# The bias of V on every other tile: from a TensorE matmul to VectorE's way out of PSUM, with a re-planned order

## The chip, the core and the metric

The kernel runs on one core of one Trainium2 chip. The metric is the device time in microseconds (us) of one execution; below is the median of several runs. The profile shows one execution, with the engines TensorE (PE; its weight loads are PEld), VectorE (DVE), ScalarE (ACT), GpSimd (POOL), and SyncE's DMA queue (SP).

## What is computed

One pre-norm layer of graph attention with a residual, on 16 graphs (batches) of 1024 nodes and 512 features, 8 heads of 64. All batches share one sparse adjacency matrix. All values are float32.

```python
h = jnp.maximum(_layernorm(x, axis=-1), 0.0)            # x: (16, 1024, 512)
q = (h @ Wq + bq).reshape(b, n, H, HD)                  # H, HD = 8, 64
k = (h @ Wk + bk).reshape(b, n, H, HD)
v = (h @ Wv + bv).reshape(b, n, H, HD)
scores = jnp.einsum('bihd,bjhd->bhij', q, k) / jnp.sqrt(jnp.float32(HD))
mask = jnp.where(adj == 0, jnp.float32(-1000000000.0), jnp.float32(0.0))
weights = jax.nn.softmax(scores + mask[None, None, :, :], axis=-1)
out = jnp.einsum('bhij,bjhd->bihd', weights, v)
x = x + out.reshape(b, n, H * HD)
```

## The kernel before

Only neighbours are computed. At the start the kernel counts each node's neighbours, ranks the nodes by that count (`degree`, `keys`, `rank_of`, `ranks`, `list_of`, `spots`), and puts them into eight tiles of 128 rows. Tile 0 holds the nodes with the longest lists, tile 7 those with the shortest. `CAPS` says how many neighbours a tile has at most (11, 8, 6, 5, 4, 3, 3, 2); the rest of the longest lists goes into "pieces", a ninth tile called -1. Tiles are taken in the order 7, 6, ..., 0 (`TILES`).

For each batch there are two halves of work.

*Projections.* A tile of x is loaded in ranked order by an indirect DMA of GpSimd (`load_x`). VectorE forms mean and variance (`stats`, `variance`, `shift`), GpSimd the power -1/2 (`power`). ScalarE norms (`norm`), TensorE flips (`flip`), ScalarE copies the flip to SBUF (`unflip`). TensorE then projects K, V and Q (`proj_kv`, `queries`). In `project` a projection is one bfloat16 matmul of `chosen` (ones in three rows) with `bias` (the bias of each projection as three bfloat16 parts that add up to it), and then four float32 matmuls, which the profile shows as eight. The three parts are made at the start by `round` on ScalarE and `remain` on GpSimd, from the bias vectors that `load_b` fetches. ScalarE takes K and V from PSUM into the tile `kvt` (`evict_kv`; the pool pkv has two PSUM banks), and SP stores it in DRAM (`store_kv`). Batch 0's rows are first projected unranked, as "batch -1" (tile names with `first`), while the ranking is still under way.

*Attention.* The slots of a tile are worked off in 14 units of up to four (`UNITS`; unit 10 is the first of tile 0, 11 the pieces, 12 and 13 the rest of tile 0). GpSimd gathers neighbours' rows of K and V by indirect DMAs (`gather`; a tile's own rows come through SP). VectorE multiplies K with the query from PSUM (`multiply`) and sums by heads (`score`), ScalarE does the exponential (`exponent`). V is weighed mostly on ScalarE, with eight activations per slot (`weigh_s`), partly on VectorE (`weigh_v`). Slots are added on VectorE or GpSimd (`fold`, `join`) and, for tile 0, on TensorE (`add_up` into the PSUM tile acc; `more` and `pass_on` bring the pieces' sums home, the matmul p_more). In the last batch most tiles are added up on TensorE. Then come `row_sums`, `scale`, `residual` and `put_out`, an indirect DMA of GpSimd.

The attention of batch b runs beside the projections of batch b+1, with three K/V tables in DRAM.

Each engine has one queue, in order. The order is made by a planner (`Plan.ordered`) in the program that builds the kernel: each operation has a length and delay (`LENGTHS`), a place (due time) from `AT` with small shifts from `FINE`, the operations it comes after, and the buffers it uses (`POOLS`). The planner takes, whenever an engine is free, the ready operation with the earliest place. So a changed place changes the order of all five queues, and nothing else.

Of the kernel before, what the change touches and what calls it, by code (L numbers as in the profile page):

```python
# [25 lines left out]
F32 = mybir.dt.float32  # L26
# [47 lines left out]
    load_x=106.07, stats=-2.83, variance=-3.87, power=-87.25, shift=-9.66, norm=-4.89, flip=-7.74, unflip=-31.23, proj_kv=-1.94,  # L74
    evict_kv=38.12, queries=-1.19, own=55.32, gather=-1.08, score=6.6, exponent=29.51, row_sums=-147.93, share=2.3,
    weigh_v=-2.68, weigh_s=90.78, fold=-2.21, join=-4.72, add_up=-1.79, direct_residual=35.08, direct_out=32.8, more=-13.17,
    pass_on=-2.39, sums=-5.19, scale=0.94, residual=-6.43, put_out=4.53, seen=40.3, zero=-27.7, zero_rate=2.38, ahead=59.92,
    early=0.74, early2=0.64, early3=0.06, first=-83.71, first_rate=7.94, v_late=15.02, key_row=-167.51, rank_row=-115.31,
    rank_d=-95.84, rank_a=-60.26, ranks=19.11, ends=25.44, list_of=68.48, tell=-159.3, spread=-73.79, others=69.47,
    spots=-98.99, long_rows=-53.11, long_0=-52.44, long=-81.28, longest=-48.97, count=59.77, pieces=-68.14, setup=-27.7,  # L80
    parts=-24.89,
)
FINE = {
    ('list_of', 5): 4.08, ('spread', 2): -8.9, (0, 'fold', 11, 2, 2): -4.64, (0, 'fold', 7, 1, 1): -1.63,
    (0, 'fold', 9, 1, 1): 4.81, (0, 'gather', 0, 1): -2.77, (0, 'gather', 10, 2): 1.19, (0, 'gather', 9, 3): -3.73,
    (0, 'join', 7): -0.85, (0, 'join', 9): 7.45, (0, 'multiply', 6): 10, (0, 'put_out', 0, 0): -1.85,
    (0, 'queries', 0, 0): -1.28, (0, 'queries', 0, 1): -0.25, (0, 'scale', 0, 1): -8.55, (0, 'weigh_s', 6, 0): 2.5,
    (1, 'fold', 1, 2, 1): 18.39, (1, 'fold', 10, 2, 2): 2.32, (1, 'fold', 11, 2, 2): -1.59, (1, 'fold', 12, 1, 1): 5.31,
    (1, 'fold', 8, 2, 2): -2.33, (1, 'norm', 2): 1.1, (1, 'norm', 3): -1.68, (1, 'proj_kv', 1, 0): -0.18,
    (1, 'proj_kv', 2, 1): -0.39, (1, 'proj_kv', 4, 1): -0.64, (1, 'proj_kv', 5, 0): 0.79, (1, 'queries', 0, 0): -0.05,  # L90
    (1, 'scale', 0, 0): -11.49, (1, 'score', 0): 0.65, (1, 'stats', 6): -0.58, (1, 'weigh_v', 12): -2.31, (2, 'flip', 6): -1.85,
    (2, 'gather', 6, 1): 9.99, (2, 'gather', 9, 0): 2.04, (2, 'multiply', 7): -1.89, (2, 'pass_on', 0): -4.55,
    (2, 'proj_kv', 5, 1): 4.27, (2, 'stats', 6): -0.96, (2, 'store_kv', 3): 0.05,
}
POOLS = dict(x=17, h=2, pht=2, hT=11, pkv=2, kvt=3, q=2, q0=1, g=6, acc=2, o=1)
GROUP = 2
JOIN = False


LENGTHS = dict(  # L100
    zeros=(0.15, 2.0, 0.0), load_w=(0.2, 2.5, 3.0), load_b=(0.6, 2.2, 0.0), load_adj=(0.2, 2.5, 1.5),
    setup=(1.0, 0.1, 0), add_bias=(0.22, 0.2, 0), join_acc=(0.602, 0.13, 0),
# [14 lines left out]
LENGTHS["fold", "POOL"] = LENGTHS["residual", "POOL"] = (1.43, 0.0, 0)  # L117
LENGTHS["gather", "SP"] = (0.1, 3.0, 1.36)
# [3 lines left out]
SHARED = ("fold", "join",  "weigh_v", "residual", "scale", "power")  # L122
# [3 lines left out]
BY_TILE = ("load_x", "stats", "norm", "flip", "unflip", "proj_kv", "evict_kv", "store_kv", "proj_q", "evict_q", "store_q")  # L126
BY_HOME = ("queries", "row_sums", "residual", "put_out", "scale", "more", "pass_on", "copy_q", "seen")
# [129 lines left out]
def planned(B):  # L257
# [17 lines left out]
    for j in range(3):  # L275
        known = [("remain", j - 1)] if j else [("parts_at",)] + [("load_b", name) for name in names]
        add(("round", j), "ACT", AT["parts"] + j, known)
        if j < 2:
            add(("remain", j), "POOL", AT["parts"] + j, [("round", j)])
# [42 lines left out]
    for n in range(-NT, tiles):  # L322
# [19 lines left out]
        for w in range(2):  # L342
# [4 lines left out]
            add(("proj_kv", n, w), "PE", e, ready, [("hT", n), ("pkv", n, w)], length=3.436 if n == -NT else None)  # L347
# [4 lines left out]
            add(("evict_kv", n, w), "ACT", e + AT["evict_kv"], ready, [("pkv", n, w), ("kvt", n)])  # L352
        ready = [("evict_kv", n, w) for w in range(2)]
        if n >= 0:
            add(("store_kv", n), "SP", p, ready, [("kvt", n)])
            continue
        add(("store_kv", n), "POOL", p, ready + [("ranks",)] + ([("store_kv", n - 1)] if n > -NT else []), [("kvt", n)])

# [5 lines left out]
    for k in range(units):  # L364
# [6 lines left out]
        q = ("q", b, t)  # L371
        if q not in q_of:
            p = i + AT["queries"]
            if t >= 0:
                ready = [("unflip", n)] + ([("round", 2), ("setup", 0), ("load_w", "q")] if b == 0 else [])
                add(("queries", b, t), "PE", p, ready, [("hT", n), q])
                if t == 0:
                    add(("copy_q", b), "ACT", p + 0.5, [("queries", b, 0)], [q, ("q0", b)])
            else:
                add(("queries", b, t), "PE", p, [("copy_q", b)] + ([("slots", 0)] if b == 0 else []), [q, ("q0", b)], length=0.86)  # L380
            q_of[q] = ("queries", b, t)
# [40 lines left out]
        elif without_tensor(b, B, home) or joined(b, B, home):  # L422
# [5 lines left out]
            summed = added  # L428
        else:
# [40 lines left out]

def is_own(u, s):

    t, first, _ = UNITS[u]
    return t >= 0 and first + s == 0


def shares_in(b, B, t):
    return t in SHARES and (b < B - 1 or t in LAST_DIRECT)


def by_vector(b, B, u):

# [853 lines left out]
```

## Time and profile before

| | |
|---|---|
| median of 11 runs | 1672.31 us (1668.26 to 1677.72) |
| the profiled execution's own time | 1675.62 us |
| its span, first to last instruction | 1673.9 us |
| granted TensorE clock, mean of the span | 0.984 |
| PE, DVE, ACT, POOL busy | 1595.8, 1482.9, 1470.5, 1272.7 us |
| DMA | 531.73 MB, 318 GB/s over the span |
| period of a steady batch | 97.7 us (p_more of tile 0 from 1280.6 to 1378.3) |

In the page's rows a slice is a fortieth of the span, and a digit the busy share in tenths. A row of a group gives line, engine, operation, output<-inputs with shapes, count | busy us, mean ns of one | idle time before it, and what ended it. A row of waits reads "engine line <- releaser: us in total, times, longest". A row of the timeline has start and duration in us, and in brackets the idle time before it. "issue" is idle time in which the engine waited for nothing that the profile shows; GpSimd has 0.30 us of it at nearly each indirect DMA.

### The profile page before, as it was taken

Reading aid. Unit: us, or ns where it says so; the run is one execution under the profiler, and the core shown is the slowest. Engines: PE = TensorE matmul, PEld = TensorE weight load, DVE = VectorE, ACT = ScalarE, POOL = GpSimd, SP = SyncE. Lnnn points to the kernel's source line nnn. Section 1 sums busy time; section 2 is a strip of 40 time slices with the busy share of each in tenths; the row PEclk is TensorE's granted clock in tenths of the full one; section 3 lists DMA queues with packets and bytes.
Section 4 is the critical chain, followed back from the end, with each engine's and each line's share of the span. In section 5 each row is a group of like instructions: output and inputs, shape, how many; then the busy total and the mean of one; then the engine's idle time right before and its main releaser. Section 6 shows DMA issues by size and latency. Waiting matters only on the chain. (4 is left out here: it accounts for less than half of the span.)

```text
span 1673.9 us, 19582 instructions
## 1 busy us (share of the span) xinstructions
PE 1595.8 (95%) x4295; PEld 737.1 (44%) x4295; DVE 1482.9 (89%) x2019; ACT 1470.5 (88%) x5479; POOL 1272.7 (76%) x1184
## 2 busy tenths in 40 slices
PE   6989999999999999999999999999999999999687
PEld 3444444444444444444444444444444444444233
DVE  6788989889898998989899898989989898998986
ACT  4359988989989898998989899898989989899976
POOL 2767777687887878788787887878787887877755
PEclk9999999999999999999999999999999999999788
DMA  6498989899898999999899998989999898999894
GB/s 229 137 333 299 336 308 338 296 355 326 317 347 304 363 325 348 327 318 348 306 357 319 349 329 306 344 321 356 323 346 332 311 350 315 358 321 332 283 330 162
DMA packets 150741, 531.73 MB, mean 318 GB/s; under 512 B 19916, under 2 KB 19916, under 8 KB 150616
## 3 DMA queue, kind: packets, MB, share of 16 engines
q0 software_dynamic: 109840, 390.70, 65.7%
q1 hardware_dynamic: 40776, 139.71, 22.9%
q8 instruction: 36, 0.59, 0.1%
q14 instruction: 89, 0.73, 0.1%
HBM read 429.51 MB, written 100.82 MB: 317 GB/s over the span
## 5 line engine op out<-in xcount | busy, mean ns | idle before, releaser
L1057 ACT ACTIVATE g<-g,weights 128x64 f32<-128x64 f32 x4696 | 1162.4, 339 | 8.0 <-DVE weights L1044 4.2
L1021 POOL DMA_INDIRECT g<-kv,index x608 | 640.1, 1053 | 247.1 <-issue 166.9
L799 PE MATMUL pq<-wq,hT 128*128 128x512 f32 x1024 | 460.3, 592 | 0.0
L1031 DVE TENSOR_TENSOR g<-g,pq 128x1536 f32<-128x1536 f32 (+2 forms) x208 | 385.7, 1871 | 82.3 <-PE pq L799 67.2
L799 PE MATMUL pk<-wk,hT 128*128 128x512 f32 x960 | 432.8, 594 | 0.0
L799 PE MATMUL pv<-wv,hT 128*128 128x512 f32 x960 | 432.3, 593 | 0.0
L1035 DVE TENSOR_REDUCE weights<-g 128x24 f32<-128x1536 f32 (+2 forms) x224 | 421.0, 1895 | 0.5
L799 PEld LDWEIGHTS pq<-wq,hT 128*128 128x128 f32 x1024 | 194.7, 190 | 218.9 <-issue 215.3
L799 PEld LDWEIGHTS pk<-wk,hT 128*128 128x128 f32 x960 | 183.2, 191 | 210.0 <-issue 206.6
L799 PEld LDWEIGHTS pv<-wv,hT 128*128 128x128 f32 x960 | 183.1, 191 | 204.6 <-issue 200.9
L1062 DVE TENSOR_TENSOR g<-g 128x512 f32<-128x512 f32 (+1 forms) x301 | 261.5, 873 | 12.4 <-ACT g L1057 11.8
L1137 POOL DMA_INDIRECT out_dram<-x,perm x128 | 147.1, 1149 | 36.9 <-issue 25.4
L744 POOL DMA_INDIRECT x<-in_x_dram,perm x128 | 141.4, 1105 | 35.4 <-issue 34.8
L1039 ACT ACTIVATE weights<-weights 128x24 f32<-128x24 f32 (+2 forms) x224 | 49.0, 219 | 104.4 <-DVE weights L1035 103.2
L1084 PE MATMUL acc<-g,ident 128*128 128x512 f32 x170 | 90.4, 646 | 35.4 <-DVE g L1062 17.1
L1062 POOL TENSOR_TENSOR g<-g 128x512 f32<-128x512 f32 x90 | 115.0, 1278 | 5.1 <-ACT g L1057 1.4
L1051 DVE TENSOR_TENSOR g<-g,weights 128x512 f32<-128x512 f32 x149 | 104.2, 700 | 0.6
L1134 POOL TENSOR_TENSOR x<-x,o 128x512 f32<-128x512 f32 x67 | 85.9, 1281 | 13.1 <-DVE o L1125 8.8
L779 ACT ACTIVATE h<-x,shift,rstd 128x512 f32<-128x512 f32 x120 | 91.1, 806 | 3.0 <-DMA x<-in_x_dram,perm 3.0
L753 DVE BATCH_NORM_STATS2 st<-x 128x6 f32<-128x512 f32 x120 | 81.9, 682 | 2.4 <-DMA x<-in_x_dram,perm 2.4
L786 PEld LDWEIGHTS pht<-ident,h 128*128 128x128 f32 x512 | 60.4, 141 | 53.3 <-issue 34.4
L786 PE MATMUL pht<-ident,h 128*128 128x128 f32 x512 | 73.4, 276 | 5.0 <-ACT h L779 4.8
(236 smaller groups left out, 1116.1 us busy)
## 6 DMA issues: line engine op xcount, KB each, us to landing
g<-kv SPq DMA_DIRECT2D x128, 512.0 KB, 6.4
kv<-kvt SPq DMA_DIRECT2D x120, 512.0 KB, 4.9
g<-kv,index POOLq DMA_INDIRECT x608, 6.7
adj<-in_adj_dram SPq DMA_DIRECT2D x8, 512.0 KB, 8.5
x_first<-in_x_dram SPq DMA_DIRECT2D x8, 256.0 KB, 8.3
x<-in_x_dram,perm POOLq DMA_INDIRECT x128, 5.9
out_dram<-x,perm POOLq DMA_INDIRECT x128, 5.4
wk<-in_L_gnn_Wk_dram SPq DMA_DIRECT2D x1, 1024.0 KB, 8.7
```

Source lines behind the costliest of these rows:

```text
L744: nc.gpsimd.indirect_dma_start(out=X[n][:], out_offset=None, in_=x_rows, in_offset=on(ap=perm[:, t : t + 1], axis=0), element_offset=b * N * D
L779: nc.scalar.activation(HN[n], X[n], AF.Relu, bias=shift, scale=scale)
L786: nc.tensor.transpose(PH[n][:, c, :], hn[:, ts(c, P)], ident)
L799: nc.tensor.matmul(pt, HT[n][:, c, :], W[name][:, c, :], start=(apart and c == 0), stop=(not apart and c == DC - 1))
L1021: nc.gpsimd.indirect_dma_start(out=G[i][:, s].rearrange("p j d -> p (j d)"), out_offset=None, in_=KV[b % len(KV)][:], in_offset=on(ap=inde ...
L1031: nc.vector.tensor_tensor(k, k, Q[b, t][:, None, :].to_broadcast([P, count, D]), ALU.mult)
L1035: nc.vector.tensor_reduce(weights[:, w, :], heads(G[i][:, :count, 0, :]), AX.X, ALU.add)
L1051: nc.vector.tensor_tensor(v, v, own.to_broadcast([P, n, H, HD]), ALU.mult)
L1057: nc.scalar.activation(v[:, h, :], v[:, h, :], AF.Identity, scale=weights[:, c + s, h : h + 1])
L1062: engine.tensor_tensor(v[:, 0:n], v[:, 0:n], v[:, first : first + n], ALU.add)
L1084: nc.tensor.matmul(ACC[b, home], owner_t if t < 0 else ident, v[:, s, :], start=(u == parts_of(home)[0] and s == 0), stop=(u == parts_of(h ...
L1137: nc.gpsimd.indirect_dma_start(out=out_rows, out_offset=on(ap=perm[:, t : t + 1], axis=0), in_=X.pop(b * NT + TILES.index(t))[:], in_offse ...
```

## The change

V's bias is left out of TensorE's matmuls for the tiles 7, 5, 3 and 1 of batches 1 to 15 (`BIAS_V`; the keys are places in `TILES`). Instead the bias of V is spread once over 128 partitions by one matmul (`spread_bias`), copied into SBUF (`copy_bias`), and added by VectorE as it takes these V tiles from PSUM. The other V tiles and K and Q stay as they were. The first `round` is planned to come after the first `power`. `AT` and `FINE` have new values throughout, so all queues are reordered, and the pool of x tiles has 16 buffers instead of 17. `PAIRED`, `FETCH`, and the GpSimd form of the bias (`bias_v`) come with the code and are switched off; of them only a column of `found0`, one more column of `p_list` and two copies of one column at the start remain.

```diff
-POOLS = dict(x=17, h=2, pht=2, hT=11, pkv=2, kvt=3, q=2, q0=1, g=6, acc=2, o=1)
+POOLS = {'x': 16, 'h': 2, 'pht': 2, 'hT': 11, 'pkv': 2, 'kvt': 3, 'q': 2, 'q0': 1, 'g': 6, 'acc': 2, 'o': 1}
...
+BIAS_V = {0: 'DVE', 2: 'DVE', 4: 'DVE', 6: 'DVE'}
+PAIRED = ()
+FETCH = False
...
+LENGTHS["evict_kv", "DVE"] = (0.602, 0.13, 0)
...
-        known = [("remain", j - 1)] if j else [("parts_at",)] + [("load_b", name) for name in names]
+        known = [("remain", j - 1)] if j else [("parts_at",), ("power", -NT // 2)] + [("load_b", name) for name in names]
...
-            add(("evict_kv", n, w), "ACT", e + AT["evict_kv"], ready, [("pkv", n, w), ("kvt", n)])
+            by = bias_by(n, "kv"[w])
+            if by == "DVE":
+                ready.append(("copy_bias",))
+            add(("evict_kv", n, w), "DVE" if by == "DVE" else "ACT", e + AT["evict_v" if by == "DVE" else "evict_kv"], ready, [("pkv", n, w), ("kvt", n)])
...
+    if BIAS_V:
+        add(("spread_bias",), "PE", AT["spread_bias"], [("round", 2), ("setup", 0)], [("pkv", "bias")])
+        add(("copy_bias",), "ACT", AT["spread_bias"], [("spread_bias",)], [("pkv", "bias")])
...
+def bias_by(n, name):
+
+    return BIAS_V.get(n % NT, "PE") if n >= 0 and name == "v" else "PE"
...
-            apart = n == -NT
+            apart = n == -NT or bias_by(n, name) != "PE"
             if not apart:
                 nc.tensor.matmul(pt, chosen[:, names.index(name), :], bias, start=True, stop=False)
             for c in range(DC):
-                nc.tensor.matmul(pt, HT[n][:, c, :], W[name][:, c, :], start=(apart and c == 0), stop=(not apart and c == DC - 1))
+                nc.tensor.matmul(pt, HT[n][:, c, :], W[name][:, c, :], start=(apart and c == 0), stop=(n != -NT and c == DC - 1))
...
-            nc.scalar.copy(KVT[n][:, j, :], PT.pop((n, j)))
+            if bias_by(n, "kv"[j]) == "DVE":
+                nc.vector.tensor_tensor(KVT[n][:, j, :], PT.pop((n, j)), bias_rows, ALU.add)
+            else:
+                nc.scalar.copy(KVT[n][:, j, :], PT.pop((n, j)))
+
+        bias_rows = const.tile([P, D], F32, tag="bias_rows", name="bias_rows") if BIAS_V else None
+
+        def spread_bias():
+            PT["bias"] = ps_kv.tile([P, D], F32, tag="pkv", name="p_bias")
+            nc.tensor.matmul(PT["bias"], chosen[:, names.index("v"), :], bias, start=True, stop=True)
+
+        def copy_bias():
+            nc.scalar.copy(bias_rows, PT.pop("bias"))
```

The new `AT` and `FINE` are tables of places (`evict_v` is 0.78, `spread_bias` -5.47) and are not shown; what they do to the order is told where it is used.

## The prediction

> **What bounds the kernel now.** I read the page's busy shares and slices first, then the engines' busy time over three steady batches, then what each engine waited for in one of them, then the timelines of the start and the end.
>
> ```profile
> PE 1595.8 (95%) x4295; PEld 737.1 (44%) x4295; DVE 1482.9 (89%) x2019; ACT 1470.5 (88%) x5479; POOL 1272.7 (76%) x1184
> ...
> PE   6989999999999999999999999999999999999687
> ```
>
> TensorE is full from the fourth slice to two slices before the end. Batches 10 to 12 (from one p_more matmul to the next; columns: stretch, its length, busy us with instructions of PE, PEld, DVE, ACT, POOL, granted clock, DMA share, GB/s):
>
> ```profile
> 1085.00:1182.90 97.90, 96.28 (x262) 44.36 (x261) 88.11 (x114) 91.06 (x343) 79.69 (x73) 1.00 0.93 333
> 1182.90:1280.60 97.70, 96.32 (x262) 44.46 (x261) 88.82 (x114) 90.96 (x343) 78.23 (x72) 1.00 0.94 332
> 1280.60:1378.30 97.70, 96.31 (x263) 44.44 (x262) 88.85 (x114) 91.00 (x343) 78.34 (x72) 1.00 0.92 334
> ```
>
> A batch takes 97.7 us, and TensorE works 96.3 of them. It loses 1.4 in small waits. The waits over two batches (us in total, times, longest):
>
> ```profile
> PE acc L1084 <- DVE g L1062: 1.9, 2, 1.0
> PE acc L1084 <- ACT kvt L814: 0.4, 1, 0.4
> PE acc L1084 <- ACT weights L1039: 0.4, 1, 0.4
> ...
> DVE g L1031 <- PE pq L799: 6.7, 2, 3.4
> ```
>
> TensorE waits once per batch for VectorE's fold of tile 0; VectorE waits 3.4 us per batch for a query. TensorE sets the pace. The Trainium skill speaks against that reading: Perfetto Trace Analysis, Identifying the Most-Contended Engine, calls matmul busy time a bad measure and wants LDWEIGHTS busy instead. By it TensorE stands at 44%, VectorE (89%) is the most contended, and a change that hands VectorE 60 more instructions would lose some of their 36 us. The row decides here: eight matmuls follow each other in 3.43 us without a break, and a shorter list on that queue ends earlier. The rule's point, that VectorE is not far behind, goes into the rivals.
>
> The two ends are different. Start (start us, duration, engine, line, idle before):
>
> ```profile
> 11.04 0.72 ACT L654 ACTIVATE scratch<-scratch,later 128x512 bf16<-128x512 f32 x1 [8.55 <-DMA scratch<-in_L_gnn_bq_dram]
> 11.85 1.15 POOL L659 TENSOR_TENSOR scratch<-scratch 128x512 f32<-128x512 f32 x1 [8.07 <-ACT scratch L654]
> 12.96 0.72 POOL L765 TENSOR_TENSOR before_told<-before_told,minus_half 128x2 f32<-128x2 f32 x1
> 13.03 0.72 ACT L654 ACTIVATE scratch<-scratch,later 128x512 bf16<-128x512 f32 x1 [1.27 <-POOL scratch L659]
> ...
> 13.91 1.52 ACT L779 ACTIVATE h_first<-x_first,before_told 128x512 f32<-128x512 f32 x2 [0.16 <-DVE before_told L769]
> ...
> 14.78 1.97 PE L786 MATMUL pht_first<-ident,h_first 128*128 128x128 f32 x8 [14.78 <-ACT h_first L779]
> ```
>
> The first norm waits for a power on GpSimd that is queued behind the bias arithmetic, and that waits for the bias DMA. End: between the last projection and the last batch's sums TensorE is starved of gathers.
>
> ```profile
> 1573.07 2.05 PE L1084 MATMUL acc<-g,ident 128*128 128x512 f32 x2 [9.62 <-issue]
> ...
> 1596.63 0.60 PE L1104 MATMUL p_more<-more,owner_t 128*128 128x8 f32 x2 [8.35 <-DVE more L1100]
> ```
>
> **The change part by part.** Durations are of one execution: span 1673.9, its own time 1675.62, which is 3.3 above the median of 1672.31. I form the difference against the span and take it off the median.
>
> 1. *Bias matmuls.* V of tiles 7, 5, 3, 1 in batches 1 to 15 loses its matmul with chosen: 15 x 4 = 60. The step from it to the next matmul is 0.216 us (1605.41 to 1605.62 in the end's timeline; the row's 379 ns contains pipeline tail). 60 x 0.216 = 13.0 us, all on TensorE's full queue. One matmul is added in the start to spread the bias (0.2): -12.7.
>
> 2. *Evictions.* 60 copies of 128x512 leave ScalarE (step 0.48 each in the chain: 29 us in all, 1.9 per batch). ScalarE had 6.7 us of slack per batch, so this earns nothing by itself. 60 additions PSUM + SBUF to SBUF come to VectorE. The nearest row has the same operand places:
>
> ```profile
> L1125 DVE TENSOR_TENSOR o<-acc,inv 128x512 f32<-128x512 f32 x22 | 15.1, 685 | 1.6 <-POOL x L1134 1.4 <-PE acc L1084 0.2
> ```
>
>    685 ns, or 0.60 from start to start in a run: 36 us, 2.4 per batch. VectorE goes from 88.6 to 91.0 of a batch that shrinks to about 96, all beside TensorE: I cost it at 0. If the cover went, it would cost up to 36. Each addition is queued behind a multiply or score of up to 2.3 us, and behind it wait a multiply and, through the two pkv banks, the next-but-one projection on TensorE. In the new order the tightest are V of tile 3 (pk of tile 2 and a flip follow: 3.65 + 0.43 = 4.1 us until TensorE wants the bank) and of tile 1 (4.9). In both VectorE's work since the last query (multiply 2.2, score 2.2, one to three pieces of 0.6) is 6 to 6.5 us, while the projection itself comes 7.1 to 7.5 after that query. So VectorE is there first, waits about 1 us, and TensorE does not wait.
>
> 3. *Does the addition block GpSimd?* No row of before shows it. SBUF — State Buffer (the Trainium skill, on the shared port pair) says that a VectorE instruction with two SBUF inputs holds a port pair against GpSimd for its whole length; ours has one in PSUM, so by the rule 0. Against it stands that indirect DMAs on GpSimd take 0.94 us in quiet and up to 1.75 in the timeline. If every addition held one up, GpSimd would lose 60 x 0.69 = 41 us, 2.8 per batch. I take 0, since VectorE's multiplies, which also read PSUM, stand beside 0.94 us gathers; 41 stays the far end.
>
> 4. *Start.* On GpSimd the first power moves ahead of the first remainder, so the constants are ready near 6.5. But ScalarE's order is still first rounding, then the two norms, and that rounding waits for the bias DMA until 11.04. Norms then start at 11.8 instead of 13.9, only the second rounding having been passed: the flip 2.1 earlier. The weights wk are in at 10.4 (issued 1.7, 8.7 to landing), so nothing new is late. Second and third rounding end about as before, and the projection that needs them comes 4 us later. -2.1, at most 8 (not reachable in this order), at least 0 if the lists and gathers, not TensorE, set the first batch.
>
> 5. *New places.* The steady order on TensorE puts tile 0's first sum three projections after the pieces' query where it was five, so it must have its fold early. Counted from the end of the query of tile 0: TensorE reaches it after 3.65 + 3.43 + 0.86 + 3.65 + 0.43 + 3.65 + 3.65 = 19.3 us; VectorE and ScalarE (multiply and score 4.4, three weighed slots 5.8 with two norms of 0.8 between, the pieces' multiply and score 4.4 beside them, fold 1.1 + 0.6) reach it near 16. Later sums have about 4 us in hand as well. So the 1.4 us of waits per batch could go. I take half: 0.6 x 12 batches = -7. Bounds: -18 (all idle of TensorE from 350 to 1550 by the slices of 50 us: 1200 - 1182.1) and +1 us or more per batch where a new order makes new waits.
>
> 6. *x pool 17 to 16.* Loads of x come about one tile later, behind the put_out that frees the buffer. In the new order the load of the next batch's first tile is issued some three units (over 15 us) before its statistics, against 5.9 us to landing: 0; without cover, about 6 us per batch. The other additions (two copies of one column in the start, under 0.2 us each; one more column in p_list) are beside longer work.
>
> 7. *The end.* The same gathers and sums in nearly the same order. The query of tile 1 stands behind one sum instead of two (VectorE waited 4.1 us for it), and the last tile's query is ahead of the last three sums. Between -5 and +5; I take 0.
>
> Sum: -12.7 - 2.1 - 7 = -21.8: span 1652, median 1650.5.
>
> **The rivals.** *Another queue takes over.* In batch 12 GpSimd's busy 78.3 and its waits of 19.0 fill the 97.7; of the waits only these two are more than issue:
>
> ```profile
> 1289.77 1.60 POOL L1021 DMA_INDIRECT g<-kv,index  x1 [1.97 <-ACT h L779]
> ...
> 1300.55 1.00 POOL L1021 DMA_INDIRECT g<-kv,index  x1 [2.10 <-issue]
> ```
>
> So GpSimd needs about 94.0 of a batch for which TensorE will need 95.4. A few slower issues and it is the bound, at 97: then 0.7 x 14 = 10 us is gained and with the start 12: 1660. For: the small margin, DMA busy at 0.93. Against: TensorE ends the waits now.
>
> *Late evictions (slower).* An addition stands behind a multiply that waits for its gather (VectorE's such waits reach 3.3 us); TensorE then waits for the pkv bank. Price: one multiply, 2.3 us, once per batch: 15 x 2.3 = 34 - 14.8 = +20: 1692. It decides from 1 us of new TensorE idle per batch, which cancels 0.86 and the start. For: VectorE's slack falls from 9.1 to 4.4. Against: the windows of part 2, and few gather waits in the steady part.
>
> *The places give all back without that*: the old waits stay and the end loses 5 to 10 us: 1662 to 1669. That TensorE executes the bias anyway is excluded: the order has no such matmul.
>
> **How the numbers follow.** TensorE still bound, waits shrunk or kept: 0.64, 1650.5, its own range 1636 to 1660. Other queue or a worse end: 0.18, 1660 to 1675. Slower: 0.18, 1676 to 1710. A measurement of this kernel tells 0.2% (3.3 us) from no change; below 1669: 0.76, within: 0.06, above: 0.18. The range 1636 to 1677 leaves out about 0.03 below and 0.17 above.
>
> **What would show it.** Right: 60 fewer matmuls with chosen and V (one more for the bias rows), 60 VectorE additions into kvt near 0.69 us, batches of 95.5 to 96.8 us, PE over 99% busy in them, first flip near 12.7. Wrong: a wait of pv or pk for DVE kvt among TensorE's waits; GpSimd without gaps while TensorE has them; a batch of 97.7 or more; a longer stretch from the last projection (1563) to the end than 110 us.

## The result: 39 us faster, 17 us more than predicted

The kernel after takes 1633.17 us (median of 8 runs, 1630.63 to 1640.33) against 1672.31: ratio 0.9769, interval 0.9754 to 0.9784, so 2.3% or 39 us less. The prediction was 1650.5, with a range from 1636 to 1677. The direction is right, but the time lies 3 us below the range: the gain is 39.1 where the sum had 21.8, and the runs below show that most of the reasons for it were not the ones given.

The profiled execution took 1628.2 us (span 1626.5), which is 5.0 below the median. Before's took 1675.62, 3.3 above its own. The two traces therefore differ by 47.4 us where the medians differ by 39.1. From the page after (busy shares, then TensorE in forty slices):

```profile
PE 1570.6 (97%) x4236; PEld 728.5 (45%) x4236; DVE 1524.1 (94%) x2081; ACT 1443.2 (89%) x5420; POOL 1250.5 (77%) x1184
...
PE   7999999999999999999999999999999999999696
```

The steady batches 10 to 12 after (stretch, length, busy us of PE, PEld, DVE, ACT, POOL, granted clock, DMA share, GB/s):

```profile
1046.20:1141.60 95.40, 95.00 (x258) 44.12 (x257) 89.58 (x118) 89.32 (x340) 77.45 (x72) 1.00 0.94 342
1141.60:1237.70 96.10, 94.91 (x257) 44.10 (x256) 92.97 (x119) 89.10 (x340) 76.34 (x73) 1.00 0.93 343
1237.70:1333.50 95.80, 94.99 (x258) 44.13 (x257) 91.62 (x118) 89.18 (x340) 76.44 (x72) 1.00 0.94 342
```

A batch takes 95.8 us instead of 97.7, TensorE is busy 95.0 of them, and VectorE has gone up by about 3 us, ScalarE down by 1.8. The removed and the added work show as the diff says (two rows of groups of after: count | busy, mean ns | idle before):

```profile
L841 PE MATMUL pv<-bias_parts,chosen 128*128 128x512 bf16 x60 | 22.8, 380 | 0.0
...
L859 DVE TENSOR_TENSOR kvt<-pv,bias_rows 128x512 f32<-128x512 f32 x60 | 40.7, 678 | 0.3 <-PE pv L843 0.3
```

An addition costs 678 ns, against the predicted 685. Where the time went is seen best with one marker that means the same work in every kernel, the end of the last K or V projection of a batch. The four stretches of before are 0 to the end of batch 1's, to that of batch 3's, to that of batch 15's, to the end:

```profile
0.00:185.20 185.20, 165.54 (x488) 81.29 (x489) 151.66 (x347) 114.11 (x333) 118.99 (x136) 0.99 0.73 259
185.20:386.20 201.00, 195.11 (x522) 89.99 (x521) 176.08 (x224) 178.83 (x671) 151.67 (x141) 0.98 0.90 324
386.20:1559.80 1173.60, 1155.75 (x3114) 532.09 (x3113) 1065.23 (x1349) 1091.67 (x4123) 936.99 (x848) 1.00 0.93 332
1559.80:1673.90 114.10, 79.40 (x176) 33.76 (x175) 89.93 (x102) 85.88 (x357) 65.06 (x61) 0.81 0.72 258
```

And those of after:

```profile
0.00:179.50 179.50, 164.22 (x480) 79.34 (x481) 158.45 (x351) 111.54 (x329) 116.36 (x133) 1.00 0.72 263
179.50:371.60 192.10, 190.32 (x513) 88.14 (x512) 184.66 (x235) 179.52 (x680) 153.45 (x142) 1.00 0.92 338
371.60:1519.90 1148.30, 1139.07 (x3070) 528.86 (x3068) 1094.64 (x1400) 1069.10 (x4066) 917.10 (x850) 1.00 0.93 341
1519.90:1626.50 106.60, 76.97 (x176) 32.18 (x176) 86.35 (x98) 83.08 (x347) 63.56 (x59) 0.87 0.71 261
```

The start gives 5.7 us, batches 2 and 3 give 8.9, the twelve steady batches 25.3 (2.1 each), and the end 7.5. The steady part can be booked on TensorE's own line, and the booking comes out: 48 bias matmuls x 0.216 = 10.4, idle time down from 17.9 to 9.2 = 8.6, and 6.3 left over in busy time, for which these rows give no cause. That is what the prediction's sum would have written. The experiments ask whether the items of this booking are also causes.

What TensorE waits for has changed. The largest waits in the steady stretch before (us in total, times, longest):

```profile
PE acc L1084 <- DVE g L1062: 11.5, 12, 1.0
PE acc L1084 <- ACT kvt L814: 3.6, 8, 0.6
```

and after, where every wait of this stretch (9.1 us) names ScalarE, most of all the copy of the query of tile 0 (`copy_q`), which the query of the pieces needs:

```profile
PE pq_-1_3911 L1070 <- ACT q L1074: 1.5, 1, 1.5
PE pq_-1_5537 L1070 <- ACT q L1074: 1.4, 1, 1.4
...
PE pk L841 <- ACT kvt L861: 0.6, 2, 0.3
```

### The profile page after: what moved, and what is told of

It reads as the page before. It is cut to its first block, busy times and chain, and to the rows that moved or that the text cites. A ratio compares the mean times of both kernels' runs of the same rounds, so it can differ in the third digit from the quotient of the medians.

```text
span 1626.5 us, 19494 instructions
## 1 busy us (share of the span) xinstructions
PE 1570.6 (97%) x4236; PEld 728.5 (45%) x4236; DVE 1524.1 (94%) x2081; ACT 1443.2 (89%) x5420; POOL 1250.5 (77%) x1184
## 5 line engine op out<-in xcount | busy, mean ns | idle before, releaser
L1093 POOL DMA_INDIRECT g<-kv,index x608 | 640.4, 1053 | 215.6 <-issue 163.9
L1107 DVE TENSOR_REDUCE weights<-g 128x32 f32<-128x2048 f32 (+2 forms) x224 | 422.7, 1889 | 0.7
L843 PEld LDWEIGHTS pv<-wv,hT 128*128 128x128 f32 x960 | 180.3, 190 | 191.4 <-issue 187.6
L1134 DVE TENSOR_TENSOR g<-g 128x512 f32<-128x512 f32 (+1 forms) x301 | 253.6, 844 | 6.0 <-ACT g L1129 5.9
L1210 POOL DMA_INDIRECT out_dram<-x,perm x128 | 136.6, 1067 | 40.5 <-issue 17.2
L788 POOL DMA_INDIRECT x<-in_x_dram,perm x128 | 132.0, 1031 | 38.5 <-issue 35.6
L1111 ACT ACTIVATE weights<-weights 128x32 f32<-128x32 f32 (+2 forms) x224 | 49.7, 222 | 77.9 <-DVE weights L1107 77.3
L1207 POOL TENSOR_TENSOR x<-x,o 128x512 f32<-128x512 f32 x67 | 86.0, 1284 | 18.7 <-DVE o L1198 15.3
L830 PEld LDWEIGHTS pht<-ident,h 128*128 128x128 f32 x512 | 63.7, 143 | 57.0 <-issue 55.2
L1157 PE MATMUL acc<-g,ident 128*128 128x512 f32 x170 | 83.3, 603 | 1.0 <-ACT g L1129 0.8
L835 ACT COPY hT<-pht 128x512 f32<-128x512 f32 x128 | 72.9, 574 | 8.9 <-PE pht L830 8.6
```

What stands on the lines that cost most here:

```text
L788: nc.gpsimd.indirect_dma_start(out=X[n][:], out_offset=None, in_=x_rows, in_offset=on(ap=perm[:, t : t + 1], axis=0), element_offset=b * N * D
L843: nc.tensor.matmul(pt, HT[n][:, c, :], W[name][:, c, :], start=(apart and c == 0), stop=(n != -NT and c == DC - 1))
L1093: nc.gpsimd.indirect_dma_start(out=G[i][:, s].rearrange("p j d -> p (j d)"), out_offset=None, in_=KV[b % len(KV)][:], in_offset=on(ap=inde ...
L1107: nc.vector.tensor_reduce(weights[:, w, :], heads(G[i][:, :count, 0, :]), AX.X, ALU.add)
L1134: engine.tensor_tensor(v[:, 0:n], v[:, 0:n], v[:, first : first + n], ALU.add)
L1157: nc.tensor.matmul(ACC[b, home], owner_t if t < 0 else ident, v[:, s, :], start=(u == added_up(b, B, home)[0] and s == 0), stop=(u == adde ...
```

## The experiments

The runs fall into five sets, each measured together on one chip: e1 to e4, e5 to e8, e9 to e12, e13 to e16, and e17 with e18. The time of the kernel before was 1687 to 1690 us in the first four sets and 1675 in the last. The chip alone does not decide this: the second and the last set ran on the same chip. So every run is told as its ratio to runs of before in its own set. The unchanged kernel after came out at 0.9757, 0.9814 and 0.9861 in three of the sets, a spread of 17 us. A pair of runs from different sets is therefore less sure than its interval says, and such pairs are marked below.

**e1: the bias matmuls alone.** The order, places and pools of before (the file is after's, with its few small additions in the start); one condition in `project`:

```diff
-            apart = n == -NT
+            apart = n == -NT or bias_by(n, name) != "PE"
```

> The order and the pools of the kernel before; only the 60 bias matmuls of V are left out (V of tiles 7, 5, 3, 1 in batches 1 to 15 goes without its bias), and ScalarE copies as before. Theory T (TensorE's queue sets the pace, and everything beyond the bias matmuls comes from the new places): -13 us at most, 60 x 0.216, and less where the shorter queue only waits longer for folds: 1659 to 1666. Theory V (the gain comes from work that left ScalarE): no more than T's share, and the batch stays near 97.9. Theory C (everything comes from the new places, the shorter queue earns nothing): within 3 us of before, the time turning up as new waits of TensorE.

Measured: 1690.45 us, ratio 1.0004 (0.9986 to 1.0022). Sixty matmuls less on the busiest queue, and nothing is gained. Three steady batches of e1:

```profile
1102.30:1200.10 97.80, 95.80 (x258) 43.75 (x257) 88.91 (x114) 90.90 (x343) 78.41 (x72) 1.00 0.93 334
1200.10:1297.80 97.70, 95.69 (x257) 43.73 (x256) 88.80 (x114) 90.89 (x343) 78.25 (x72) 1.00 0.93 333
1297.80:1395.50 97.70, 95.77 (x258) 43.75 (x257) 88.81 (x114) 90.90 (x343) 78.49 (x70) 1.00 0.93 333
```

These batches take 97.7 to 97.8 us as before, and none of e1 is shorter; others take 98 to 100, so that the mean over the twelve steady batches is 98.3. In the three, TensorE works 0.55 less and stands 2.0 instead of 1.4. So in the order of before TensorE, 98.6% busy, did not set the pace: something else took 97.7. The trace shows a candidate, and no more than that. GpSimd has a gather that stands about 2.1 us idle in most batches. In one batch of before (first line) and in one of e1 (second) the profile puts this down to a query projection of TensorE:

```profile
1200.71 0.99 POOL L1021 DMA_INDIRECT g<-kv,index  x1 [2.08 <-PE pq L799]
```

```profile
1217.91 1.00 POOL L1132 DMA_INDIRECT g<-kv,index  x1 [2.08 <-PE pq L882]
```

In most other batches a wait of 2.1 us about there is put down to "issue", as in the prediction's line at 1300.55. From that gather GpSimd has no gap over 0.6 us for the next 89 us (e1, until 1307). Ahead of the gather stand 18 us of TensorE (from p_more to that query), and the one projection of V among them is of a tile that keeps its bias. A loop that passes through TensorE only there wouldn't feel the removed matmuls. That this loop sets the batch is not shown.

**e2: VectorE's additions in the order of before.** As e1, and at the place of ScalarE's copy:

```diff
-                nc.scalar.copy(KVT[n][:, j, :], PT.pop((n, j)))
+                nc.vector.tensor_tensor(KVT[n][:, j, :], PT.pop((n, j)), W["v"][:, 0, :], ALU.add)
```

> The order and the pools of the kernel before; the 60 bias matmuls of V are left out and VectorE evicts these tiles by an addition, standing where ScalarE's copy stood. As the rows of the bias don't fit beside the pool of 17, a chunk of the weights of V, of the same shape, is added in their place. Theory T: the additions stand in a queue that wasn't ordered for them, so 0 to 15 us slower than the same order without the additions: 1660 to 1680. Theory V (relief of ScalarE is worth time in any order): clearly faster than the same order with ScalarE's copies, by 10 us or more: 1640 to 1655.

Measured: 1701.86 us, ratio 1.0082 (1.0056 to 1.0108): 13 us slower than e1 (8 to 19). The largest of TensorE's waits in e2:

```profile
PE pv L880 <- DVE kvt L898: 17.3, 15, 1.3
```

That is the prediction's slower rival, late evictions, at its place. The whole bias move, put into the order of before, loses time.

**e5, e7, e8: is it GpSimd?** e5 is before, unchanged. e8 is before, and e7 is e1, without GpSimd's four additions of x and o per batch:

```diff
             add = G.pop(b * NU + parts_of(t)[0])[:, 0, 1, :] if shares_in(b, B, t) else O.pop((b, t))
+            if not shares_in(b, B, t) and not residual_by_vector(b, B, t) and b < B - 1:
+                return
```

> The kernel before, unchanged, for its trace on the same chip as the three beside it. Every theory: ratio 1.000, a steady batch of 97.7 to 98.2 us with TensorE busy 96.3 of it.

> As e1 (the order before, the 60 bias matmuls of V and so that bias left out, ScalarE copies), and with the four GpSimd additions of x and o per batch left out in batches 1 to 15 (the rows of tiles 3, 2, 1 and 0 go out without x + o): GpSimd is 4 x 1.29 = 5.2 us lighter per batch. Theory G (the order before was paced at 97.7 us by GpSimd's chain of gathers and its waits for g buffers, with TensorE only just behind): the batch falls to TensorE's 95.5 plus small waits, 95.5 to 96.3, so 22 to 33 us under before: ratio 0.980 to 0.987. Theory T (a loop of TensorE and VectorE, waits of sums for folds and of VectorE for queries, paces it, GpSimd not): batch 97.7 as in e1, ratio 0.998 to 1.002.

> The kernel before with its bias matmuls, and only the same four GpSimd additions per batch left out. Theory G: GpSimd no longer paces, TensorE does with 96.3 busy: batch 96.4 to 97.0, 11 to 20 us under before, ratio 0.988 to 0.994, and 10 to 13 us above e7: with GpSimd out of the way the bias matmuls cost their 0.86 us per batch. Theory T: as before, ratio 0.998 to 1.002. If it comes out equal to e7 and both are faster, then TensorE is not second in line and the bias matmuls are hidden by something else.

Measured: e5 1.0007 (0.9986 to 1.0028), e7 1.0013 (0.9990 to 1.0036), e8 1.0017 (0.9992 to 1.0043). Theory G fails as it was put: 5.2 us less on GpSimd in each batch gain nothing in all. The batches show why it isn't simply false. In e8 some fall to 96.2 us, which no batch of e5 does, and in e7 to 95.1; others then take 98 to 99.6. The mean over the twelve steady batches is 97.85 us in e5, 97.65 in e8, 98.33 in e1, 97.12 in e7. This fits an order that is held by several loops of nearly the same length, where a single relief moves the waits; the loops themselves are argued, and which of them holds which batch stays open. DMA, 0.93 busy in the steady part, was not tried by itself. It was not at a ceiling there, since after moves 341 GB/s in its steady stretch where before moves 332.

**e3, e4, e13: the order of after, with the parts of the bias move put back.** e13 has both back, e3 the bias matmuls only (first line of the diff), e4 ScalarE's copies only (the second change):

```diff
-            apart = n == -NT or bias_by(n, name) != "PE"
+            apart = n == -NT
...
-            if bias_by(n, "kv"[j]) == "DVE":
-                nc.vector.tensor_tensor(KVT[n][:, j, :], PT.pop((n, j)), bias_rows, ALU.add)
-            else:
-                nc.scalar.copy(KVT[n][:, j, :], PT.pop((n, j)))
+            nc.scalar.copy(KVT[n][:, j, :], PT.pop((n, j)))
```

> The order of the kernel after, with the 60 bias matmuls put back on TensorE as well: the bias of V goes in twice on these tiles, once by TensorE and once by VectorE. Theory T: the batch is 4 x 0.216 = 0.86 us longer, 13 us in all: 1644 to 1648, and the other 26 us of the gain stay. Theory B (in the new order another queue, VectorE or GpSimd, sets the pace): less than 4 us is lost, 1633 to 1637, and TensorE's waits shrink instead. A loss well over 13 us would say that the order lives on the time that the bias matmuls gave free.

> The order of the kernel after, without the bias matmuls, but ScalarE copies these 60 tiles of V at the place where VectorE added (their bias is left out). ScalarE has 60 x 0.48 = 29 us more, VectorE 36 us less. Theory T: neither is the bound, so within 5 us of after, 1630 to 1640. Theory V (what earns is ScalarE's relief): 1650 or more, the copies queued late behind the norms and exponentials of ScalarE, with waits of TensorE for kvt. Theory D (VectorE's 36 us cost the kernel after something): faster than after by 3 us or more, 1620 to 1629.

> The order of after, instruction for instruction, but V of every tile keeps its bias matmul on TensorE, and ScalarE copies where VectorE added: nothing of the bias move is left, only the places (and the x pool and the start that go with them). Theory P (the places are the gain, the bias matmul is free in either order): within 5 us of e4's kernel, ratio 0.981 to 0.990, and at most 10 us over after on the same chip. Theory T (TensorE's 0.86 us per batch count): 13 us over e4's ratio, 0.992 or more. Theory B (the places need VectorE's eviction): 1.00 or more, as e12 with its own order had it.

With them e16, the kernel after in the set of e13 (e6 and e9 are the same in other sets):

> The kernel after, unchanged, beside e13 to e15 on one chip: ratio 0.976 to 0.987, the pieces' query waiting 0.3 to 2.6 us for ScalarE's copy in each batch.

| order of after, and | V of 4 tiles copied by ScalarE | by VectorE, adding |
|---|---|---|
| bias matmuls on TensorE | e13: 0.9867 (0.9851 to 0.9884) | e3: 0.9786 (0.9760 to 0.9812) |
| without them | e4: 0.9846 (0.9809 to 0.9882) | e16: 0.9757 (0.9739 to 0.9775) |

The order alone, with nothing of the bias move, gains 1.33% or 22 us (20 to 25). The whole bias move in that order gains another 1.10%, 19 us (14 to 23; the medians of e13 and e16 lie 17.3 apart). Both come from one set. Their traces place them: from e13 to e16 the start, batches 2 and 3 and the end differ by 1.2 us at most, and the steady stretch is 14.1 shorter (1167.0 to 1152.9).

Inside the move the eviction is the larger part: e13 to e3, 0.0081 or 14 us (8 to 19) with all bias matmuls still on TensorE; e4 to e16, 0.0089. The matmuls are the smaller: e13 to e4, 3.5 us (-3 to 10), e3 to e16, 5 us (-1 to 10). These four pairs cross sets, but e3 and e4 were in one: there taking the copies off ScalarE beats taking the matmuls off TensorE by 0.0060 (0.0015 to 0.0105), 10 us. The mean steady batch of the traces agrees: 97.4 us in e13, 97.1 in e4, 96.7 in e3, 96.1 in e16 (96.8 and 96.7 in e9 and e6).

The times that the expectations of e3 and e4 name were worked out from a before of 1672, and their set had 1689.62; e3 took 1653.57 and e4 1660.07. Of e13's theory P the ratio came, and "within 5 us of e4's kernel"; its "at most 10 us over after" did not, with 17 to 19.

TensorE's waits say the same. In the stretch from 383 to 1540 us all of them in e13 (16.3 us), e3 (10.7) and e4 (19.0), and all but 0.9 of the 13.4 in e16, name ScalarE. The largest of e13:

```profile
PE pk L880 <- ACT kvt L900: 6.8, 9, 0.8
PE pq_-1_8829 L1109 <- ACT q L1113: 2.1, 1, 2.1
```

and the same row in e3:

```profile
PE pk L880 <- ACT kvt L900: 0.7, 3, 0.3
```

With four V tiles per batch off ScalarE, K's copies come in time; this row is 6.1 us of the difference, and the rest has no such row. Without the bias matmuls but with ScalarE's copies (e4) TensorE waits 2.7 us longer for 10.4 less work.

**e6, e9, e10: the matmuls once more, in one set.** e6 and e9 are after, unchanged, and e10 is e3's kernel beside e9.

> The kernel after, unchanged, for its trace on the same chip. Every theory: ratio 0.975 to 0.978, a steady batch of 95.4 to 96.1 us with TensorE busy 95.0 of it.

> The kernel after, unchanged, for its trace on the same chip as the three beside it. The chip decides how much of the gain shows: ratio 0.974 to 0.988, a steady batch of 95.5 to 96.8 us with TensorE busy 95.0 of it.

> The kernel of e3 again (the order of after, the 60 bias matmuls also on TensorE, so that bias goes in twice on these tiles), beside after on one chip. Theory T (in the new order TensorE paces): 13 us over e9, 10 to 16, ratio 0.006 to 0.010 above e9's. Theory G (the loop through GpSimd paces in both orders, and the new order only has a shorter one): within 4 us of e9.

Measured: e6 0.9861 (0.9809 to 0.9914), e9 0.9814 (0.9768 to 0.9860), e10 0.9819 (0.9789 to 0.9850). e6 misses its range. e10 lies 0.0005 over e9, 1 us (-9 to 10), nearer to theory G's 4 than to theory T's 10 to 16, though G's loop through GpSimd is not shown by that. In the steady part of e9 the pieces' query waits up to 2.6 us for `copy_q`, in that of e10 at most 1.6, and TensorE's waits sum to 16.7 and 11.1: part of the matmuls seems to fill waits that are there anyway.

**e11: VectorE's additions twice.**

```diff
+                nc.vector.tensor_tensor(KVT[n][:, j, :], PT[n, j], bias_rows, ALU.add)
                 nc.vector.tensor_tensor(KVT[n][:, j, :], PT.pop((n, j)), bias_rows, ALU.add)
```

> The kernel after with each of the 60 evictions by VectorE done twice: 36 us more on VectorE, 2.4 per batch, nothing else changed. Prediction's step 2 (VectorE's additions lie beside other work): within 5 us of e9. If VectorE is now in the loop: 20 to 36 us over e9, with TensorE waiting for kvt or for folds.

Measured: 0.9927 (0.9909 to 0.9945), 19 us over e9 (11 to 27 by the intervals) for 36 us of work. VectorE is not beside the path; about half of what is added to it comes out in the time. In the two traces the steady part grows by 8.9 us: TensorE stands 4.3 longer, and is 4.6 longer busy with the same matmuls, at a granted clock of 0.99 instead of 1.00 (the last section has what a wait can do to the clock). TensorE's waits of e11 don't name VectorE, though:

```profile
PE pq_-1_8828 L1110 <- ACT q L1114: 3.3, 1, 3.3
PE pq_-1_4743 L1110 <- ACT q L1114: 2.7, 1, 2.7
```

ScalarE's exponentials wait for VectorE's scores. In two batches of after (1141.6 to 1333.5 us):

```profile
ACT weights L1111 <- DVE weights L1107: 11.5, 9, 2.0
```

The weighed slots and the copy of the query stand behind the exponential in ScalarE's queue, so a delay of VectorE can arrive at TensorE as a wait for ScalarE: a wait is put down to the last member of such a chain. That e11's delay took this way is argued, not shown; in sum the exponentials wait for the scores no longer in e11 (49.2 us in the steady part) than in e9 (49.6).

**e12: the weights alone.** Here the planner places ScalarE's copies itself:

```diff
-BIAS_V = {0: 'DVE', 2: 'DVE', 4: 'DVE', 6: 'DVE'}
+BIAS_V = {}
```

> Only the places: all weights of the new order, the x pool of 16 and the start as after, but V of every tile keeps its bias matmul on TensorE and is copied out by ScalarE. Theory P (the places are the whole gain, the bias move worth nothing): ratio within 0.003 of e9's. Theory T + P (the places end the loop of 97.7 us, then TensorE's floor with bias of 96.3 holds): 13 to 20 us over e9, about 1655 where after has 1640. Theory B (the places only pay with the bias moved, since the copies return to a full ScalarE): within 5 us of before, or slower.

Measured: 1773.17 us, ratio 1.0510 (1.0492 to 1.0527), worse than all others. Theory B's outcome, but e13 shows that its reason is not right: the order of after works without VectorE's eviction. The weights don't: with another list of operations the same weights give another order, with a batch of 105 us. `AT` and `FINE` are not a property of the kernel that can be carried over.

**e14, e15: the copy of the query earlier.** In batches 0 to 14 of the order of after:

```diff
+        order.remove(("copy_q", b))
+        at = order.index(("queries", b, 0))
+        while order[at][0] != "weigh_s":
+            at += 1
+        order.insert(at + 1, ("copy_q", b))
```

> The kernel after, with one change: ScalarE's copy of the query of tile 0 moves from behind three and more weighed slots and a copy of K to just behind the first weighed slot after that query, in batches 0 to 14. Theory L (in the new order the last wait of TensorE is that of the pieces' query for this copy, 0.3 to 2.6 us per batch, and that sets the batch): it goes, and the batch falls toward TensorE's 95.5: 5 to 18 us under after on this chip. Theory G (the loop through GpSimd sets it): no change within 4 us, the wait of TensorE turning up elsewhere.

> As e14, and the 60 bias matmuls on TensorE as well (that bias goes in twice on these tiles). Theory L: with the wait gone TensorE paces, and the matmuls cost what the prediction's step 1 says, 10 to 13 us over e14. If they stay free here too (within 4 us of e14), TensorE isn't the bound even without that wait.

Measured: e14 0.9781 (0.9745 to 0.9817), e15 0.9814 (0.9795 to 0.9833), beside e16's 0.9757. The wait for the copy is gone in the steady batches, and this one is in its place (e14, 383 to 1540 us), as theory G had it:

```profile
PE pk L887 <- ACT kvt L907: 10.5, 15, 2.9
```

Theory L fails: nothing is gained by moving one copy within ScalarE's queue. It seems to be the queue as a whole that is late. e15 lies 6 us (-1 to 12) over e14: that leaves room for some of the 13 us of the matmuls, not for all that the prediction's step asks for.

**e17, e18: the two ends.** e17 is after up to the last projection of K and V, and in the order of before from there. e18 puts the first power, norms and flips back behind the first remainder and the second rounding:

```diff
+    moved = [("shift", -NT // 2), ("norm", -NT), ("norm", 1 - NT), ("flip", -NT), ("flip", 1 - NT)]
+    rest = [key for key in order if key not in moved]
+    at = rest.index(("round", 1)) + 1
+    return rest[:at] + moved + rest[at:]
```

> The order of after up to and including the last projection of K and V (of the last batch), and from there on the order of before: only the last 107 us differ from after. From the traces of before and after (114.3 and 106.7 us from the end of that projection to the end): 7 us over after, ratio 0.982 to 0.991, the stretch 112 to 116 us long. If the old order of the end costs nothing by itself (the end was only late because of what came ahead of it), the stretch stays 105 to 109 us.

> The order of after, but the first power, norms and flips stand behind the first remainder and the second bias rounding, as in before. The prediction's step 4: the first flip 2.1 us later and the end 2 us later, ratio within 0.002 of after. If the start is not on the path of the first batch (the lists and gathers are): the first flip later, the first sum of pieces (184.9 to 195 us in after) unmoved, and the time unchanged.

Measured: e17 0.9770 (0.9751 to 0.9790), e18 0.9761 (0.9741 to 0.9782); neither can be told from after's 0.9769 by its time, and e17's ratio is better than was expected. What follows is read from single executions. By the marker, e18 reaches batch 1's last projection at 183.7 us and e17 at 180.3. Its first flip comes at 13.79 instead of 9.69, but 1.9 of these 4.1 us are the bias transfer, which landed later in that execution (the first rounding starts at 10.06 instead of 8.21). So the old start costs 3.4 us at most. The old end takes 111.7 us (e17), the new one 106.6 in after and 108.2 in e18: 3 to 5 us. In e17 the old wait of the end is back:

```profile
1555.92 0.60 PE L1228 MATMUL p_more<-more,owner_t 128*128 128x8 f32 x2 [8.17 <-DVE more L1224]
```

In after it is gone, and the sums of the pieces wait instead:

```profile
1534.93 2.07 PE L1157 MATMUL acc<-g,owner_t 128*128 128x512 f32 x2 [10.17 <-POOL g L1134]
...
1549.51 0.36 PE L1177 MATMUL p_more<-more,owner_t 128*128 128x8 f32 x2 [0.22 <-DVE more L1173]
```

## Why the prediction was wrong

*"TensorE sets the pace."* This is the step that failed. The prediction read it from 96.3 busy of 97.7 and from eight matmuls without a break. e1 takes it away for the order of before: the shortest batches stay at 97.7 with TensorE at 95.75. In the order of after, 13 us of matmuls put back on TensorE cost 1 to 6. A queue that is 98.6% busy still has 1.4 us per batch in which it waits for others, and what it waits for may be a loop that doesn't contain the work that is removed. The sum came out too small because what it put at nothing, ScalarE's relief, and what it put low, the new order, paid more than the matmuls fell short of their place in the sum: matmuls -12.7 against -1 to -6; evictions 0 against about -14; start, places, pool and end -9.1 against -22 (e13).

The Trainium skill's rule that was put aside at this place (Perfetto Trace Analysis, Identifying the Most-Contended Engine: the engine with the highest occupancy, TensorE apart) was also read on the wrong rows. Over the whole span it names VectorE by its 89%; in the prediction's own three steady batches it names ScalarE, with 91.0 of 97.7 us against VectorE's 88.8. ScalarE is the engine whose relief paid in the order of after and that TensorE's waits name there. The rule would not have been enough: in the order of before the same relief lost 13 us (e2), and e7 and e13 show no one engine to be the bound.

*Step 1, bias matmuls, -12.7.* Over-sized. It is nothing in the order of before (e1, 1.0004), and 1 to 6 us in that of after (e10 over e9 and e15 over e14 within one set; e4 under e13 and e16 under e3 across sets), with no interval that reaches 13.

*Step 2, evictions, "ScalarE had 6.7 us of slack per batch, so this earns nothing by itself", VectorE at 0.* Wrong on both sides, and by luck the sizes make up for step 1: about -14 us net, by e13 to e3 across sets, or the 19 of e13 to e16 less the 1 to 6 of the matmuls. ScalarE's 6.7 us of slack was its mean over a batch, while the copies of K and V and of the query are wanted at fixed times behind weighed slots of 2 us each; that this is the reason is argued from the waits for kvt (6.8 us in e13, 0.7 in e3). VectorE's cost is real (e11), but less than what ScalarE gets back. The price depends on the order: the same eviction loses 13 us in the order of before (e2).

*Step 3, no blocking of GpSimd.* Borne out as far as it can be seen: 608 gathers at 1053 ns in before and in after.

*Step 4, start, -2.1.* The first flip was to come near 12.7 and came at 10.53, 4.25 us earlier than before: 2.0 because the bias transfer that the first rounding waits for landed earlier in that execution (the rounding starts at 9.05, before at 11.04), and the other 2.2 by the norms' new place, nearly as worked out:

```profile
10.53 1.97 PE L830 MATMUL pht_first<-ident,h_first 128*128 128x128 f32 x8 [10.53 <-ACT h_first L823]
```

By e18 against e17 the moved norms are worth 3.4 us at most, and the times do not tell the two apart.

*Step 5, new places, -7.* The mechanism was seen, that the sums of tile 0 no longer wait for their folds (11.5 us in the steady stretch, none after). The size is wrong. In e13, where only the places are new, the steady part is 7.2 us shorter than in e5, as large as the step, but batches 2 and 3 are 7.9 shorter, and the prediction's bound looked only at the time from 350 us on. There, before, TensorE stood 5.9 us and ran at a clock of 0.98; after, 1.8 us and 1.00. Nearly all of the standing was two waits for a fold, and after each the matmuls took twice their time, at a granted clock of 0.50 (214.1 to 217.4 and 309.7 to 313.0 us):

```profile
214.58 2.08 PE L1084 MATMUL acc<-g,ident 128*128 128x512 f32 x2 [2.90 <-DVE g L1062]
...
309.89 2.07 PE L1084 MATMUL acc<-g,ident 128*128 128x512 f32 x2 [2.76 <-DVE g L1062]
```

The new order took both waits away, and with them two stretches of 3.3 us at half clock, which by these figures is an estimated 3 us. In e13's trace its gain lies in all four stretches: against e5, 8.3 us in the start, 7.9 in batches 2 and 3, 7.2 in the steady part and 4.5 in the end. The pair crosses sets, and 27.9 us is more than the 22 of the ratio.

*Step 6, the x pool, 0.* Not tried apart; it is part of e13.

*Step 7, the end, 0.* It was -3 to -5 (e17, single executions), inside the given -5 to +5.

*The rivals.* Late evictions by VectorE are real in the order of before (e2, 17.3 us of waits for kvt), and no wait of after's steady stretch names one. "Another queue takes over" was right that TensorE is relieved in vain beyond a point, and not borne out in the queue: the waits name ScalarE, not GpSimd.

The signs that were to show the steps right were there: 60 matmuls fewer, additions at 678 ns, batches of 95.8 us, TensorE 99% busy, an end under 110 us, and the first flip even earlier than told. None of them could tell the cause, since all hold as well where the order and ScalarE's relief shorten the batch and TensorE merely follows.

## What to carry to other kernels

A busy queue's removed instruction is worth its length only if the queue waits for nobody: with 1.4 us of waits per batch left, first ask which loop ends those waits and whether the removed work lies in it. Booking the gain on the busiest engine's line afterwards came out here and proved nothing; a run with only that part of the change tests it. And where the order is planned, try the new order with the old operations: here it made more than half of the gain, and the same eviction was worth about -14 us in one order and +13 in the other.

## What the hardware showed that was not expected

*A short idle time can cost twice.* The two matmuls of the pieces' query take 1.13 us after 1.19 us of idle time (after, first line) and 2.06 after 2.57 (e9):

```profile
1224.51 1.13 PE L1070 MATMUL pq_-1_10415<-q,owner 128*128 128x512 f32 x2 [1.19 <-ACT q L1074]
```

```profile
1246.69 2.06 PE L1070 MATMUL pq_-1_10415<-q,owner 128*128 128x512 f32 x2 [2.57 <-ACT q L1074]
```

So a wait of 1.4 us more made the pair end 2.3 later. The granted clock was 1.00 from 1224.5 to 1225.5 us in after and 0.54 from 1246.6 to 1248.4 in e9. Not each such wait does this: earlier in e9 the same pair takes 1.12 us after 2.46, at a clock of 1.00 (473.8 to 476.0). TensorE: Matmul & The Clock Gate (the Trainium skill, Part 1) has the clock halved after an idle window of about 3.4 us. Here it was halved already behind 2.57.

*Engines that stop for nothing.* In the sets in which before took 1687 to 1690 us instead of 1672 to 1675, runs of short instructions have gaps without any wait that explains them. VectorE at the end of the lists, in before's profile and in e5's (the second is held 1.26 us by an instruction that took 0.16 and was long done):

```profile
79.19 0.17 DVE L981 COPY weights<-number 128x8 f32<-128x8 f32 x1
79.40 0.16 DVE L980 TENSOR_REDUCE number<-free 128x1 f32<-128x6 f32 x1
```

```profile
84.96 0.17 DVE L981 COPY weights<-number 128x8 f32<-128x8 f32 x1 [1.26 <-DVE number L980]
86.36 0.16 DVE L980 TENSOR_REDUCE number<-free 128x1 f32<-128x6 f32 x1 [1.23 <-DVE weights L981]
```

By the end of this list e5 is 12.4 us behind before, most of the difference between the two executions; 7.8 of it arise within the list. On ScalarE, weighed slots that run without a gap in after (32 activations in 7.73 us) have three in e9:

```profile
1241.02 0.59 ACT L1129 ACTIVATE g<-g,weights 128x64 f32<-128x64 f32 x2 [0.46 <-issue]
1241.76 0.35 ACT L1129 ACTIVATE g<-g,weights 128x64 f32<-128x64 f32 x1 [0.16 <-issue]
1242.48 3.21 ACT L1129 ACTIVATE g<-g,weights 128x64 f32<-128x64 f32 x13 [0.37 <-issue]
```

They come right ahead of the copy for which TensorE then waits 2.57 us. From 383 to 1540 us, ScalarE's idle time that the profile puts down to "issue" is 16.0 us in e5, 20.8 in e6, 15.1 in e9 and 15.3 in e16; before, after and e17 have none. After gains 1.4 to 2.4% from set to set, and such gaps in the queue on which its order leans may be a reason (e6 has the most and gains the least), but e16 has as many as e9 and gains the most. So the shares of the parts were measured in sets with these gaps, and for the 39 us of the first comparison they are only likely.

What stops the engines is open. Late instructions would be a candidate: Runtime: NRT & Kernel Launch (the Trainium skill, Instruction fetch mechanics) says that each engine fetches its program by DMA in blocks while it runs, mostly hidden. The traces speak against it at these places: the DMA queues of the kind "instruction" (1.3 MB in e5's span) moved nothing from 82 to 95 us in e5 and from 1239 to 1243.2 in e9.
